# Two Fourier-attention layers on one core: x of batch 0 requested in pairs of units, first statistics of batch 1 on ScalarE, other ones and another order

## The chip, the core and the metric

The kernel runs as one program on one core of a Trainium2 chip. The metric is the time of one execution on the device, in microseconds; before the change it is 398.73 us, the median of 3 runs (398.27 to 398.82). The core has TensorE (PE, with its weight loads PEld), VectorE (DVE), ScalarE (ACT), GpSimd (POOL) and SyncE (SP). SyncE does nothing but issue DMA transfers; ScalarE issues some as well.

## The reference, cut to what matters

The input x has 2 batches, 56 channels and 128 x 128 points. Two layers of the same form, with weights of their own, are applied one after the other: x = x + layer(gn(x)). In a layer each channel is a token, a field of 128 x 128 points:

```python
# B, K, H, W, A = (2, 56, 128, 128, 8); N = batch and channel
def gn(v):       # one mean and variance for each batch and each group of 4 columns,
    ...          # over all 56 channels and all 128 rows
    return (v - mean) / sqrt(var + 1e-5)
# layer(t):
xa = t.reshape(B * K, 1, H, W)
xn = inorm(xa, g1, b1)                     # inorm: per field, over its 128 x 128 points
k, q, v = (fno_layer(xn, ...) for the K, Q and V weights)           # 8 heads each
attn = softmax(einsum('baks,bals->bakl', q, k) / sqrt(H * W))       # 56 x 56 for each head
out = fno_layer(attn @ v, P weights)
att = inorm(out + xa, gan, ban)
an  = inorm(att, g2, b2)
h   = fno_layer(an, M0 weights, norm=True, act=True)                # act: gelu
h   = fno_layer(h, M1 weights, norm=True)
y   = inorm(h, gmo, bmo) + att
# fno_layer: irfft2(complex weights times the 32 x 16 kept modes of rfft2(x)) + b,
#            inorm if norm, plus a 1x1 skip, gelu if act
```

What matters below is that the very first step of each layer, gn, needs the sums and the squares over a whole batch: until all of a batch's x is there, nothing of it can be scaled.

## The kernel before, in words

**Data.** x lies in one SBUF tile X2, for each batch as 8 *units* (n = 0 to 7), each with 8 rows of points for two halves c = 0, 1 of the planes. Half c takes partitions 64c to 64c + 55, one for a channel; partition 64c + 56 holds ones, which is why 32 partitions of X2 are set to 1.0 (`row_of_ones`) before the channels 28 to 55 are loaded over part of them. So a unit of batch 0 is loaded by pieces: channels 0 to 27 for four units at a time (448 KB), channels 28 to 55 for one or two units (112 or 224 KB), and each piece must wait for the setting to ones where it overlaps. Batch 1 is loaded by 32 pieces of 112 KB.

**First stage.** `turned(0, b, n, stats)`, noted `turn0b.n`, transposes unit n on TensorE into a pair of PSUM banks (columns become partitions), copies it to P[b], and takes its statistics for each column. Before the change VectorE does that with two bn_stats of 448 elements each, from P or, for units 6 and 7 of batch 0, from PSUM. Only units 1 and 2 of batch 0 (`SUMMED`) have them from ScalarE: a copy with a running sum, and a square over the same PSUM with a running sum. `modes_chain(0, b)`, noted `modes0b`, collects them (VectorE, unit 0 or 1 of that note), averages groups of 4 columns by a matmul with the constant `group` (modes00's unit 2), takes the power -1/2 on GpSimd, and then transforms the plane: for batch 0 with scaled transform weights `fwg`, P being scaled by four ScalarE pieces afterwards (`plane_scaled`). `gram0b`, `scores0b`, `values0b`, `soft0b`, `mix0b`, `heads0b` and `norms0b` are the attention; `gelu0b`, `hchain0b` and `end0b` the two layers behind it; `prep0` and `prep1` prepare the weights of each layer. The second layer has the same notes with a 1 (`turn10`, `modes10` and so on), and takes its statistics on ScalarE for both batches.

**Order.** The program is first recorded as a list of numbered units of work, each with the engines that may do it. `ORDER`, a long text, then fixes in which order units are issued and by which engine: a word is the step to the next unit's number and the letter of its engine (V, S, G, T for VectorE, ScalarE, GpSimd, TensorE, Q for SyncE; a small v has the next GpSimd unit wait for it). Each engine works through its part strictly in that order; between engines the dependencies are found by the framework. `PLACES` gives the PSUM bank of each intermediate. A transfer is issued by SyncE or ScalarE, and a later transfer may have to wait in the queue for an earlier one to land.

**Ones.** `awake(m)` is a matmul of a tile of ones with m columns, whose result nobody reads. `AWAKE` lists them with a number, which is only their name: `awake.108` is the one listed as 10.8. There are 84, with 26,112 columns together; each leaves two matmul records. They stand in TensorE's order between the real units.

**Constants.** The constants lie in one tile, loaded by `load_const` in parts: part 0 the identity, part 1 `fw`, `group` and `fx` (144 KB), part 2 small masks (56 KB), part 4 `gw` (64 KB), and others. The weights of layer 0 come as two pieces of 272 KB (`stage`), the scalars as two of 63 KB (`sm`).

All instructions pass through the one line L243 that issues a unit, so the profile's groups are told apart by their tiles.

Of the kernel before, what the change touches and what calls it, by code (L numbers as in the profile page):

```python
# [21 lines left out]
0V 1Q 2S 5G 1V -5Q 12S 1Q -7G 1V 7S 1Q -17S 3S 7G 1V 7S 1Q 2Q -16V 7G 1Q 7S 2S -18S 25T 3T 75Q -60T -24T 14T -2T  # L22
-5T 4T -6T 86G 47V -41G -96T 1T 36T -34T 88V -2G 10Q -12Q 6V -77T 119G -50Q 7G 3G 95G -42T 1S 2T 1S -150T 23T
61Q 109G -41T -124T 125S -61V 63T -123T -17T 121V 15V -55Q 60S -16T 8S -53Q 63T -142T 125S 2T 11V -144T 88Q 63T
-79Q 62S -33Q -94T 140V 3V -34Q 16V -135T 5T 151V -55Q 37S 17S -58Q 88G -28T 1S -62Q 129V 1v 1T 1V -230T 154S
-134T -12T 223G 2S 6T -7V 4G -107G -10Q 70v -87Q 138V -2V -134Q 138T -8T 7T 4T -112V 57G 1G -110Q 24Q 138V 1T 4T
-56V 1v -73Q 74T -26T 730G -789Q 128V 24T -15V -11V 14V -2T 3T 1T -50V 56S 6T -61v 1G 1G -108Q 109G 1G -10V -74Q
10G 126S 6T 1T -168Q 155S -54V -81Q 52S -55Q 81V 64S -62V 2T 8T 46S -158Q 167V -92V 86G -145Q 5Q 84S 66T -6S 7T
1T 1T 1T -109V 49V 1V -3V -96Q 143S -224T 82Q 141G 41S -185Q 174V -169Q -14Q 195V -4V -1V 2v 7G -206Q 68T -55Q
-92T 159T 1S 328Q -232v 231Q -230V -63V -46V 110T 2V 1G -158Q 62T 1S 116G -278T 481Q -373V 85T 2T -114Q 426Q  # L30
-505T 192S -105Q 63T -7V 12V -4S 10V 42G -51V 4T 1S 1V 98S -112T 1S 1V 198V -61G -30S -57V -2V 101T -38T 16T 5G
-1T -19S 38S -193Q -96T -15T 353T 1V 1G -344T 290T -11S -85V -2V 3T 82V 68V 2S 1S -350T 266V -162Q -112T 288T
207Q -492T 288V 1T 64V -55S -8T 66V 4T 3T -158V 88T 64v 149Q -145V 1T 4T -64V 62V 1T 4T -10V -1V 19T -173G 97V
2S -100V 164V 1T -201G 137V 1T 73S 111Q -183S 73T -88T -174V 263T 1T 1T 1T -117V -1v 105V 1T 1S 12T 1T 1T 11G
-191V 89T -23V 102S 22V -9V -14S -100V -10V 112S -207V 96V 143V -115S 119V -97T 62S 32V 1v -113S 188Q -177T 36G
45S 1T -81V 122T -39V 1G -98S 21T 1T -5T -103V 274Q -170V 100V 4V -99T -8T 1V 83S 1T 16T 3V -100T -305T 406T
-96S 72S -221v 251G 11S 60Q -76S 13T 1S -34V -76V 6T -4T 2S -3v 97G -91V 1T 1V 1G 95T 83Q -89T -312Q 227V 1T 1V
-326T 395G 15S -89V 1T 1S 4G 90T -104S 2S 13V 1V 1T 93T 1S -12V 1T 1T 67Q -149V -1v 141Q -54S 8V -1G -88T 1V
161Q -239G 218T -62S -19G 30S 1v -93T 1V 148T -55T 1S 8T 1T 1T 39V 27Q -407Q 386V 1T 5S 386G -385S 11Q -242G
135V -63V 543V 2V 1v -448T 1V 90Q -81T 60T -59V 60V -15S 18Q -1Q -16S 19T 1V -73T 1V 87Q -2Q -84T 72T 1S 1S 13T  # L40
-265G 255S 1S 13Q -138G 53v 7V -421T -26T 389G 57T 2T 79T -78V 68Q -67G 76Q 354G -358V -80T 2S -1S 43T 1S 36Q 1Q
4V 1T -75V 76S -75T 1V 1G -6V 7V 1v 82Q 1Q -2Q -50T 1S 53T 6T -7Q 2V -14S 18Q -108S 4G -442T 545Q -1Q -13S -515T
178G 349Q 5V 126Q 16Q -233T 2V -1V 2v 72S -105T 122T -530T 409S 61T 1V -28T 1V 87S 1S -102T 218Q -217S 60T 182Q
# [12 lines left out]
769T 1V 9V 15Q -797T 898S -88T 10V -9V -233Q -576T 805T 1S 1S 20T 10V 65T 1V 2T 1V -134G 5T 127T 4T -130S 60G
-59S 63Q -259Q 324T 4T -308Q 29Q 164T -15v 16S 102G 10V 1T -269Q 145T 1S 61V -50S 114V 1T 8T 1T -36G 15V -58T
71S -281Q 195V 72G 19T -131S 61G -39V 19V -14T 108T 1T -90T 82v -1S -71S 1S 80T 1T 1T -325Q 346G -129V 5T -2Q
106T -307Q 214S -19S 1S 15Q 85V 1V 36V -67V 85T -22V -21V -93S 113V 2V -167Q 41S 1S 147S -20V 17T 1S -41V 44T 1S
-135Q 183V 1T -211Q -189Q 331v 70V -94T 35T -145Q -227Q 326V -308Q 321V 93G -92G 34T -33S 1T 91V 4S -149T 70T 4T  # L60
-370Q 442S -208Q 345Q -136V 1V -254Q 107V 75V 11S 66T -68S -956T 594Q 433T -253Q 162V -6v -129Q -178Q 402V 1T 4T
-2V 1T 4T 137Q -139V 1T -82S -346Q 224Q 206V -157G -57Q 126G 97T 1T -118V 109T 1S -85G 88S -437Q 436S -117V 27V
1T 3V 1T 198Q -216v 19T 11G -202Q 282T 1T 1T -255Q -226Q 471S -246Q 260v -3T 1T 1T -267Q 238G -55V 1S 56G -252Q
157G 40V 1T 71S 32V -50V 19T -279Q 290S 1T 39T -165V -134Q 177S 1T 7T 1T 1T 91V -90T 95v -104V 5T 169Q -316Q
315Q -70S 18S -38V -1V 19G -470Q 379S 74G 1V -82T 83T 16T -15S 21V -3v 7G 63Q -164V -180Q 365Q -192V 112T 1S
-478Q 374T 93T -9V 10v 2G -91V -3S -223Q 48Q 185V -8T 2T 162Q -111S -430Q 17Q 369T 85S -91V 90T -14v -95T -389Q
402V 2S 11V -6G 101T -312Q 308T -90G -6V 7V 1V 1T 82V -101S 21V 86S 4S -9T 1T -83v 95V -1G -88T 1V 59G 99Q -240G
167T -122S 126S 1v -4S -219G 117T 1S 152Q -216G 217T 1V -142T 169Q -3Q 1Q -166V 93T 53T 1V 35Q -419Q 420Q -89S
8T 1T -105G 150T 5S 1S -157v 152S 35Q -34S 17Q -242G 170T 36V -35V -174V -150Q 332T 1T 1S 57T 1V 21Q 3Q 3Q -22T
1V 38Q -19Q -88T -45V 95T 1S 19T 1S 18Q -14S -3S 33Q -99v 70S 9T -395Q 396V 27Q -290G 268T 1V -84T 2S -1S 45T 1S  # L70
38T 1S -96T 112Q -54T -105G 62V -14V 115T -102T 2T -60G 66V 37V 38S -80V -58G 141S 1S 9T -428Q 397T 1S -5T -57G
96Q -1Q 4V 69Q -163T 83Q 2Q 3V 7T 45Q -144V 5V 1G -311Q 312V 1v 49S 5T 1V -69S -4G 110S 1S -92T -317Q 319V -32T
170Q -148T 1S -1133T 1141V 2v 92S -21T 1S -68T 1V -37S 34T 1V 90S -26T 63Q 1Q 22Q -14T -218G 214Q 3Q -70S 5T 1V
20T 1S 41Q -46T 50V -11Q 4T 1V 27Q -2Q -68S -164G 169T 1V 44T 1S 1S -220V 175T 1T 1V 56T -10S 2T -1S -46V 74Q
-251v 238T -13S 3Q 2Q 3V 3Q -58T 2S 54Q 5V -19T 1S 19T -14T -43V -2V 4V 2V 40V -43T 2T 2T 65Q -64V 1G 62Q -61V
1V -13S 81Q -6Q -13S -48G 52S 10T 1V -14S 4S -3T 1S 15Q 17Q -29T -53V 64Q -10S 13T -63T 1S 172S -28S -86Q 5V
111v -124T 1V -68G 13T 2V 66T -1315T 1320S 1S -73v 4V 80Q 76S 16G -169T 1V 60S 20T -14T 1S 7T 96G -109S -64T 65T
9Q 83S -84Q -7S 14Q 2Q -1Q 3V -8Q 2V 7T 5S -89V 173T 6V -5V 9Q -93S 87Q -107T 1V 14S 1S 69G -64T -4T 1V 69G 19Q
-18T 6V 1Q -23G -50S 1T 1V 73Q -8V 4Q -37S -31T 1T 2V 21G 5S 37Q -34G -23V 24T 6V 4Q -2Q 26Q -65S 2T 6T -1369T
1389G -23V 4T 23V 1Q 2Q 7S 39Q -38G -9Q 29Q -59S 6T 36T -35V 2V -1G 2V 33V -44S 12G 1v -1372T 1434Q 5Q -35Q 2Q  # L80
-14Q 33Q -1436T 1419V 32Q -35Q 22Q -1423T 1392Q -2Q 16Q -37T -11G 12v 38Q -36T 1V 95S -1479T 1414Q 66G -98v 4T
1V 61Q -30Q -30T 1V 70T 24T 1V -68Q -1406T 1471S 1G 5V -2Q -17S 2S 1G -11T 12T 4V 10S -25T 1V 7G 20S -1Q -37T
-1T 2T 25Q 1S -13V -1S -1Q 3Q -1453T 1460V 2S -1470T 1469Q -18V 2S -1Q -4V 2S -1446T 1445Q -1446T -2T -7T 4T 1T
1463S
# [98 lines left out]
SUMMED = (1, 2)  # L183
# [85 lines left out]
def fno_layers(ctx: ExitStack, tc: tile.TileContext, x, out, weights, small, const):  # L269
# [89 lines left out]
    def begin():  # L359
# [15 lines left out]
        for g in (0, 4):  # L375
            for c in range(2):
                load_x("QS"[c], 0, c, 0, 28, g, 4)
# [927 lines left out]
```

## Time and profile before

| | before |
|---|---|
| median of 3 runs | 398.73 us (398.27 to 398.82) |
| the profiled execution: time, span | 397.13 us, 395.3 us |
| mean granted TensorE clock | 0.978 |
| PE busy, share of the span | 371.3 us, 94% |
| DVE busy | 325.8 us, 82% |
| ACT busy | 253.1 us, 64% |
| POOL busy | 199.6 us, 50% |
| HBM read, written | 24.29 MB, 14.68 MB |
| matmuls of ones (168 records) | 63.5 us |

The durations below come from the profiled execution, and its span begins with the first instruction. A row of the timeline has the start, the length, the engine, the operation, what it writes and reads, the count of merged instructions, and in brackets the idle time before it and what ended that. Rows with ACTq or SPq are DMA transfers being issued by a queue; their length is the time in which they were issued, not the transfer's own.

### The profile page before, as it was taken

The numbers are of one execution on the slowest core, as the hardware profiler recorded it, in microseconds if no ns is written. First come the engines' busy times: TensorE is split into PE (matmuls) and PEld (weight loads), VectorE is DVE, ScalarE is ACT, GpSimd is POOL, SyncE is SP. The second block draws the span as 40 slices with busy tenths as digits, with TensorE's granted clock in tenths as the row PEclk, the third lists the DMA queues.
The fourth block names the chain that finished last, engine by engine and source line by source line (L and its number), as shares of the span: only waits on it lengthen the run. The fifth ranks groups of instructions, "written<-read, shape, count | busy, mean of one in ns | idle before, by whom it ended". The sixth has DMA issues, their size and how long they took to land.

```text
span 395.3 us, 14788 instructions
## 1 busy us (share of the span) xinstructions
PE 371.3 (94%) x6380; PEld 251.9 (64%) x6380; DVE 325.8 (82%) x583; ACT 253.1 (64%) x446; POOL 199.6 (50%) x207
## 2 busy tenths in 40 slices
PE   8789999999999999999999999999998999888895
PEld 4465687498657655667766696597575555456453
DVE  7554899999799897799869999778988888986972
ACT  0164788526947979873886798765559958993400
POOL 9942529421565566426628811434556440397460
PEclk9868999999999999999989999999999999999999
DMA  7989700300005355200120346620045324312756
GB/s 165 220 194 202 211 9 2 111 3 3 2 2 163 89 139 157 83 2 26 57 63 2 97 126 195 211 62 2 2 119 161 118 74 133 83 36 90 224 178 225
DMA packets 21317, 39.93 MB, mean 101 GB/s; under 512 B 4612, under 2 KB 5380, under 8 KB 21252
## 3 DMA queue, kind: packets, MB, share of 16 engines
q1 hardware_dynamic: 20002, 35.25, 31.6%
q10 hardware_dynamic: 1250, 3.74, 3.4%
q8 instruction: 50, 0.82, 0.9%
q14 instruction: 15, 0.12, 0.1%
HBM read 24.29 MB, written 14.68 MB: 99 GB/s over the span
## 4 chain that ended last, share of the span: by engine, by line
PE 63%; DVE 15%; ACT 9%; issue 4%; DMA 4%; POOL 3%; SPq 0%; ACTq 0%; DVEq 0%; POOLq 0%
PE psum L243 63%; ACT P L243 5%; DVE P L243 5%; DMA X<-x 3%; DVE WU L243 3%; DVE WT L243 2%; DVE X L243 2%; POOL X L243 2%; ACT psum L243 2%; DMA xr<-store 1%; DVE f L243 1%; POOL P L243 1%; ACT WT L243 1%; ACT L243 1%; SPq L243 0%
## 5 line engine op out<-in xcount | busy, mean ns | idle before, releaser
L243 PE MATMUL psum<-ones 128*128 128x256 f32 (+3 forms) x168 | 63.5, 504 | 2.0 <-DVE ones L243 1.0
L243 POOL TENSOR_TENSOR X<-X,gvr 128x1024 f32<-128x1024 f32 x20 | 47.2, 2375 | 18.8 <-DVE P L243 7.8
L243 PEld LDWEIGHTS psum<-C,P 32*128 32x128 f32 (+4 forms) x1124 | 40.4, 159 | 19.0 <-issue 4.9
L243 PEld LDWEIGHTS psum<-P 128*64 128x64 f32 (+1 forms) x1568 | 48.5, 138 | 4.9 <-ACT P L243 2.3
L243 PE MATMUL psum<-P 128*64 128x56 f32 (+1 forms) x1568 | 50.9, 223 | 0.5 <-ACT P L243 0.5
L243 PE MATMUL psum<-C,P 32*128 32x128 f32 (+4 forms) x1124 | 48.2, 252 | 2.3 <-DVE X L243 0.9
L243 DVE SCALAR_TENSOR_TENSOR X<-psum,cols,xr 128x1024 f32<-128x1024 f32 x32 | 40.1, 1270 | 5.0 <-PE psum L243 2.2
L243 PEld LDWEIGHTS psum<-ones 128*128 128x128 f32 x168 | 30.4, 213 | 21.6 <-issue 9.2
L243 ACT COPY P<-psum 128x1024 f32<-128x1024 f32 (+4 forms) x38 | 32.7, 893 | 11.8 <-PE psum L243 10.3
L243 ACT ACTIVATE P<-psum,cols 128x1024 f32<-128x1024 f32 x32 | 35.2, 1111 | 6.0 <-PE psum L243 5.5
L243 PE MATMUL psum<-X,BTx 57*64 57x512 f32 x256 | 34.6, 612 | 1.9 <-ACT psum L243 1.0
L243 ACT ACTIVATE psum<-P 128x1024 f32<-128x1024 f32 x32 | 33.0, 1031 | 0.7
L243 ACT COPY WT<-psum 128x896 f32<-128x896 f32 x30 | 26.7, 906 | 10.0 <-PE psum L243 9.7
L243 DVE STREAM_TRANSPOSE P<-psum 128x448 f32<-128x448 f32 (+1 forms) x24 | 28.8, 1230 | 2.6 <-PE psum L243 2.6
L243 POOL TENSOR_TENSOR P<-P,X 128x1024 f32<-128x1024 f32 x12 | 28.0, 2374 | 5.1 <-ACT P L243 2.9
L243 PE MATMUL psum<-P,C 128*64 128x112 f32 (+2 forms) x296 | 29.1, 381 | 1.1 <-DVE gc L243 0.4
L243 PEld LDWEIGHTS psum<-C,X 56*128 56x128 f32 x512 | 20.4, 152 | 11.7 <-issue 7.9
L243 ACT ACTIVATE P<-xf,uc 128x56 f32<-128x56 f32 x112 | 26.8, 332 | 1.5 <-PE psum L243 1.5
L243 POOL TENSOR_TENSOR X<-P,X 128x1024 f32<-128x1024 f32 x10 | 23.5, 2378 | 7.6 <-DVE P L243 4.2
L243 PE MATMUL psum<-C,X 56*128 56x56 f32 x512 | 24.4, 243 | 3.1 <-DMA X<-x 2.2
L243 ACT ACTIVATE P<-P,sh,gv 128x1792 f32<-128x1792 f32 x12 | 21.9, 1874 | 7.6 <-PE psum L243 5.3
L243 DVE SCALAR_TENSOR_TENSOR P<-P,hs,psum 128x1024 f32<-128x1024 f32 x20 | 24.6, 1272 | 2.2 <-PE psum L243 2.0
(236 smaller groups left out, 713.4 us busy)
## 6 DMA issues: line engine op xcount, KB each, us to landing
xr<-x SPq DMA_DIRECT2D x64, 112.0 KB
store<-X SPq DMA_DIRECT2D x64, 112.0 KB
xr<-store SPq DMA_DIRECT2D x64, 112.0 KB
X<-x SPq DMA_DIRECT2D x34, 112.0 KB
out<-P SPq DMA_DIRECT2D x32, 112.0 KB
out<-P SPq DMA_DIRECT2D x8, 224.0 KB
out<-P ACTq DMA_DIRECT2D x8, 224.0 KB
stage<-weights SPq DMA_DIRECT2D x4, 272.0 KB
```

What stands on the lines that cost most here:

```text
L243: done = getattr(engines[letter.upper()], method)(*args, **kw)
```

## The change

1. *x of batch 0.* SyncE asks for half c = 0 and ScalarE for c = 1, pair of units by pair: channels 0 to 27 of units 0 to 3, then channels 28 to 55 of units 0 and 1, then 2 and 3, then channels 0 to 27 of units 4 to 7, then channels 28 to 55 of 4 and 5; units 6 and 7 are asked for by SyncE alone. The settings to ones go in the same order. ScalarE's first activation (`mhalf`), which brings its table load, comes behind its second request instead of behind its last. ScalarE issues 5 transfers of x instead of 7. No transfer of batch 1, of weights or of scalars is asked for before the last of batch 0; constant part 1 is asked for after it, with eight others between.
2. *Statistics.* For batch 1 of the first layer all eight units get ScalarE's summing copy and summing square; the 16 bn_stats and their bn_aggr go, and `modes01` adds the sums up like the second layer does.
3. *Ones.* 62 instead of 84, with 20,224 columns, at other places.
4. *Order.* `ORDER` and `PLACES` are new as a whole. The units are the same but for those named. In batch 0 the units are transposed in the order 1, 0, 3, 2, 4, 5, 6, 7 instead of 2, 3, 4, 5, 0, 6, 1, 7; some other units change engine, among them four products of scores00 from GpSimd to VectorE, one set of 16 small products there from ScalarE to GpSimd and one to VectorE, and two scalings of X2 from VectorE to GpSimd.

```diff
 ORDER = """
-0V 1Q 2S 5G 1V -5Q 12S 1Q -7G 1V 7S 1Q -17S 3S 7G 1V 7S 1Q 2Q -16V 7G 1Q 7S 2S -18S 25T 3T 75Q -60T -24T 14T -2T
...
+0V 1Q 1S 1S 1S 1V 1G 1Q 1S 1V 1G 1Q 1S 1Q 1S 1V 1G 1Q 1S 1V 1G 1Q 1Q 1Q 1Q 18T -8T -2T 65G 2G 39V -103T 58V -62T
...
 AWAKE = [(0, 512)] * 9 + [
-    (10.8, 512), (14.4, 512), (15.3, 384), (17.4, 256), (18.7, 256), (20.6, 384), (23.1, 512), (24.0, 256),
...
+    (8.1, 512), (9.0, 128), (10.0, 512), (10.9, 128), (12.6, 384), (15.9, 512), (16.8, 128), (18.4, 256),
...
         clear("V", ones, 1.0)
-        for g in (0, 4):
-            for c in range(2):
-                load_x("QS"[c], 0, c, 0, 28, g, 4)
-            if not g:
-                load_const("S", 0)
+        load_x("Q", 0, 0, 0, 28, 0, 4)
+        load_x("S", 0, 1, 0, 28, 0, 4)
+        load_const("S", 0)
         S.activation(mhalf, ones[:, :2], AF.Copy, scale=-0.5)
-        for g in range(0, 8, 2):
+        for g in (0, 2):
             for c in range(2):
                 row_of_ones("VG"[c], 0, c, g, 2)
-        for g, n in ((0, 2), (2, 2), (4, 2), (6, 1), (7, 1)):
             for c in range(2):
-                load_x("QS"[c], 0, c, 28, K, g, n)
+                load_x("QS"[c], 0, c, 28, K, g, 2)
+        for c in range(2):
+            load_x("QS"[c], 0, c, 0, 28, 4, 4)
+        for c in range(2):
+            row_of_ones("VG"[c], 0, c, 4, 2)
+        for c in range(2):
+            load_x("QS"[c], 0, c, 28, K, 4, 2)
+        for c in range(2):
+            row_of_ones("VG"[c], 0, c, 6, 2)
+        for g in (6, 7):
+            for c in range(2):
+                load_x("Q", 0, c, 28, K, g, 1)
...
-        if L == 0 and b == 0 and n in SUMMED:
-            k = 72 + SUMMED.index(n)
+        if L == 0 and (b or n in SUMMED):
+            k, m = (n, 8) if b else (72 + SUMMED.index(n), 2)
             S.activation(grid(dst, 2), p[:, :, :448], AF.Copy, accum_out=acc[:, k : k + 1])
-            S.activation(p[:, :, :448], p[:, :, :448], AF.Square, accum_out=acc[:, k + 2 : k + 3])
+            S.activation(p[:, :, :448], p[:, :, :448], AF.Square, accum_out=acc[:, k + m : k + m + 1])
         elif L == 0:
             copy("SV", grid(dst, 2), p[:, :, :448])
-            k = 2 * n if b else 2 * [i for i in range(8) if i not in SUMMED].index(n)
+            k = 2 * [i for i in range(8) if i not in SUMMED].index(n)
             with work.unit():
                 for s in range(2):
-                    V.bn_stats(stats[:, k + s, :], p[:, s, :448] if b == 0 and n >= 6 else grid(dst, 2)[:, s])
+                    V.bn_stats(stats[:, k + s, :], p[:, s, :448] if n >= 6 else grid(dst, 2)[:, s])
...
-            if L == 0:
-                V.bn_aggr(mv, flat if b else flat[:, :72])
+            if L + b == 0:
+                V.bn_aggr(mv, flat[:, :72])
                 V.tensor_scalar(mv[:, 1:2], mv[:, 0:1], mv[:, 0:1], mv[:, 1:2], ALU.mult, ALU.add)
-                if b == 0:
-                    V.scalar_tensor_tensor(mv, mv, 0.75, rest, ALU.mult, ALU.add)
+                V.scalar_tensor_tensor(mv, mv, 0.75, rest, ALU.mult, ALU.add)
             else:
                 V.tensor_reduce(mv, flat[:, :16].rearrange("p (a n) -> p a n", a=2), AX.X, ALU.add)
                 V.tensor_scalar(mv, mv, 1.0 / (N * K), None, ALU.mult)
+            if L == 1:
                 V.tensor_scalar(mv[:, 0:1], mv[:, 0:1], nm0, None, ALU.add)
```

More of the change, by code (lines that the diff above doesn't have):

```diff
@@ L27 @@
[L27 to L31, printed above, removed]
@@ new lines @@
+19V -120S 119V 2V -80S 87v -127S 333Q -411Q 67T 1S 1S 343Q -212G -180Q 62T 331Q -291V 1V 57V 1G 1S 248Q -251S
+-239T 180V -37S 1S 37V -178T 2T 61Q 64T 1S 1S 111T 1S 15T 3V 1T -262T 5T 247V 16V -80V 90T 1S -16V 4V 62V -64v
+65T 1V 1G 1V 3S -1S 3G 2V 147Q -148V -249Q 93T -176T 273T 1S -280T 357T -92T 3V 1T 1T 66V -3V 7T 3T -159v 87T
+70V 1T 4T -101G 99V 1T 4T -262Q 157G 38V 1S 64V 1T 11T 1T -2V -262V 185G -96G 165V 1T -67V 1T 1S 66S 9T 1T 1T 1T
+1T 1T -94S 191Q -277V 191V -10V 9V -20S -103V -106V 314Q -106S -103V 35T -139V 35S 5V 180S 98Q -113S 16T -220V
@@ new lines @@
+24V 1G 124T -145T 1V 145S 1T 1V -138V 14Q -603T 567T 1S 1S 32Q 16T 10V 237T -250T 251S -137T -113S 1S 2V 111T 2S
+-1S -102V 4Q -20Q -36T 1S 1S 41v 247T 2V -278G 142T 3V 4V -5S -741T 631T 1S -630T 742V 132V -128V -108T 1S -8S
+9S 98V -152G 157T 2T 2T 1V 1G -139T 1S 1S -621T 759V 9G -8V 1G -751T 599T 1S -10T 1S 283V -122V 1T -13V 15V
+-141Q -13S -609T 762v 7T 1V -774T 889G -285S 291v -888T 764T 1V -769T 893T 1V -7G 8G -130T 1S 114V 21G -5V 4S
+-889T 888S -108T 10V -789T 760T 20V -19V -175Q -2Q 186V -205Q -574T 601Q -597T 600Q 222T 10V -837T 585Q 243V
@@ new lines @@
+-7Q 5V 1Q -99G -61G 164T -98G 97Q -1Q 3V -98V 60T 18S -412Q 395S -5T 1S 42T 45Q -137v -3T 1V 1G 2V 92S 1S -446Q
+407T 1V 16T -395Q 325T 2V -337Q 475Q 16Q -155V 2v 71T 58Q -61S 4S -105T 125S -124S 36T 1V -3T 1V -332Q 252G
+-259Q 409T 65Q -45S -167G 164T 45Q -5Q -439Q 298T 150T -48S 45Q -146S 150V -46T 37Q 44Q -21Q 1Q -22T 1V 25Q -64S
+1T 1V -1231T 1275T -213G -4G 222S -72V 24T 1T 48S 1T -47V -1S 42S 7S 9Q 18Q -69V 55T -2Q 1Q 2V -20S -218G 231T
+-4Q 5V -55T 2S 40T 1S 19T 5S 1S 8Q -73V 6V -2V 56S -15T 1V -48V 5T -2S 71Q -496Q 246G 256Q -73T 2T 1V 2V 64T
@@ L85 @@
+5Q -20Q -15Q 34Q -44T 1V 71T -49Q -14Q 7Q 43Q -13Q -1430T 1411V 4Q -1Q -2Q 52S 11S 1G 3T 4V 2S -1Q -29T -1456T
+1458T 23V 2S -1Q -15S -8V 1Q 1S 5G -52Q 48V 7T 1V -7Q 5G 5V 2S -4Q 1S -24T -1T 2T 4V -1449T 1451S -1Q -4V 2S 22Q
+-1464T 1441Q 13S -1458T 3T
 """
 PLACES = [int(c) for c in (
[L88 to L89 removed]
@@ L92 @@
+    "0622420246603002046550664764204460234426540020576462660620420026464"
 )]
```

106 lines of the change are left out of this document (45 added, 61 removed), and 17 rows, old and new, of the table AWAKE.

## The prediction

> **What bounds the kernel now.** I read the page first, then the chain of waits, then the head in the timeline, then tables by stretch of time.
>
> ```profile
> span 395.3 us, 14788 instructions
> ```
>
> The profiled execution took 397.13 us, so 1.8 us lie outside its span; the median of the runs is 398.73 us, 1.6 us above it. I make the sum against 397.13 and add 1.6 at the end. The chain of waits (start, length, what):
>
> ```profile
> 5.09 13.20 DMA X<-x
> 18.31 0.33 ACTq L243
> 18.68 1.28 ACT L243
> ...
> 20.17 1.70 ACT P L243 x3
> 21.92 16.37 PE psum L243 x127
> ...
> 39.39 17.39 PE psum L243 x397
> 56.81 5.14 PE psum L243 x105
> 61.96 49.52 PE psum L243 x830
> ```
>
> The head is a story of its own: until 18.6 us the chain lies in x transfers and in ScalarE's queue, which issues them; then come the table load and ScalarE's first copies, then TensorE. From 39.4 to 111.5 us TensorE hardly pauses. The timeline of the head:
>
> ```profile
> 2.55 16.10 ACTq L243 DMA_DIRECT2D X<-x  x7
> ...
> 29.84 1.11 PE L243 MATMUL psum<-C,X 56*128 56x56 f32 x16
> 30.88 3.44 PE L243 MATMUL psum<-ones 128*128 128x256 f32 x6
> 30.98 1.16 DVE L243 BATCH_NORM_STATS2 stats<-psum 128x6 f32<-128x448 f32 x2 [2.16 <-PE psum L243]
> ...
> 34.25 0.71 PE L243 MATMUL psum<-C,X 56*128 56x56 f32 x16
> 34.89 0.38 PE L243 MATMUL psum<-mv,C 128*128 128x2 f32 x2
> ...
> 37.28 1.71 PE L243 MATMUL psum<-P,fwg 128*32 128x448 f32 x16
> ```
>
> ScalarE spends 16.1 us issuing seven requests for x, because a request waits in its queue until an earlier one has landed. Its copies stand behind that, so the last of batch 0's eight transposed units starts at 29.84 us, and the matmul that averages the statistics (psum<-mv,C, in modes00) only at 34.89, behind three ones (30.88 to 34.3) and the first unit of batch 1. The first scaled transform (psum<-P,fwg) follows at 37.28. These two are my milestones. By stretches (length, then busy time of PE, PEld, DVE, ACT, POOL, then granted clock, DMA share, GB/s):
>
> ```profile
> 0.00:20.00 20.00, 16.40 (x65) 8.78 (x65) 12.65 (x10) 1.31 (x2) 18.75 (x14) 0.91 0.84 192
> 20.00:40.00 20.00, 18.41 (x165) 11.76 (x169) 10.93 (x27) 10.22 (x17) 6.89 (x17) 0.74 0.87 199
> 40.00:60.00 20.00, 19.97 (x448) 15.59 (x448) 18.00 (x49) 15.51 (x28) 8.70 (x25) 1.00 0.39 103
> 60.00:80.00 20.00, 20.00 (x235) 11.43 (x235) 19.18 (x43) 12.96 (x28) 12.41 (x16) 1.00 0.19 56
> 80.00:100.00 20.00, 20.00 (x519) 17.48 (x520) 18.84 (x29) 9.54 (x21) 4.00 (x4) 1.00 0.01 3
> ```
>
> The DMA engines are full (share 0.84 and 0.87) for 40 us, at 192 and 199 GB/s; afterwards VectorE is busy 90 to 96% beside a full TensorE, part of which are ones. In the head what matters is which bytes come first; behind it, TensorE and VectorE together.
>
> **The head: x by pairs, the table load first.** Batch 0 of x is 56x128x128 floats, 3.67 MB; with the identity (64 KB) 3.73 MB. Before, a piece of batch 1, weights and constants were mixed in. Now nothing else is asked for ahead of batch 0. At 192 GB/s it is moved by 3.73/0.192 = 19.4 us. From the last byte to the waiting engine I allow 2 us, an estimate (0 to 4: no row shows it alone): 21.4. ScalarE issues five requests for x instead of seven, its table load comes ahead of most of them, and it is free long before. The mean cannot come right then: the request for the "group" constant used to be SyncE's eighth and now stands behind eight others that follow batch 0. Their sizes:
>
> ```profile
> X<-x SPq DMA_DIRECT2D x34, 112.0 KB
> stage<-weights SPq DMA_DIRECT2D x4, 272.0 KB
> ...
> C<-const_all SPq DMA_DIRECT2D x1, 144.0 KB
> sm<-small SPq DMA_DIRECT2D x2, 63.0 KB
> C<-const_all ACTq DMA_DIRECT2D x1, 64.0 KB
> C<-const_all SPq DMA_DIRECT2D x1, 64.0 KB
> C<-const_all SPq DMA_DIRECT2D x1, 56.0 KB
> ```
>
> Two pieces of weights, two of x, two of small, three constants (64, 56 and its own 144 KB): 1158 KB, 1.19 MB. So 4.92 MB must be in: 3.84 MB by 20 us, 1.08 MB more at 199 GB/s is 5.4 us: 25.4, with the 2 us 27.4. The other way to the mean is shorter: last transposes at 21.4 + 1.1, then three ones of 1280 columns (the three at 30.88 have 1280 too, 3.44 us) make 25.9. So psum<-mv,C starts at 27.4 instead of 34.89. To psum<-P,fwg it is 2.4 us as before; one unit of batch 1 now stands between them, whose last request lies three requests (336 KB, 1.7 us) behind the constant: 29.1 plus its 0.71. I take 30.3 against 37.28: **-7.0**. With no landing lag -9; with 4 us, and TensorE late behind ones at half clock, -4. SyncE's queue pays: units 6 and 7 are asked for by SyncE alone, which delays batch 1's requests; bytes, not issues, set their time, and the units wanted early (0 and 3) are asked for first, so I cost that at nothing. If unit 7, wanted near 39 us, is late, everything behind it on TensorE waits, about 1 us.
>
> ```profile
> 24.00:32.00 8.00, 8.00 (x75) 5.98 (x74) 4.49 (x9) 4.24 (x8) 2.80 (x3) 0.50 0.81 189
> ```
>
> TensorE ran this stretch at clock 0.50, although it was busy throughout. The Trainium skill, "TensorE: Matmul & The Clock Gate", Part 1, says that the clock falls to half after an idle window of about 3.4 us and comes back after a busy one; a full 8 us at half are longer than that. By the rule the new wait for x of units 4 and 5 would leave the three ones at half clock, and without it they would take less. Both end before the constant lands, so the sum stays.
>
> **First statistics of batch 1 on ScalarE.** VectorE loses the 16 bn_stats of batch 1; each of the eight units becomes a summing copy and a summing square on ScalarE, as two units of batch 0 already are:
>
> ```profile
> 28.86 0.92 ACT L243 ACTIVATE P<-psum 128x896 f32<-128x896 f32 x1 [2.19 <-PE psum L243]
> ...
> 30.61 0.19 ACT L243 ACTIVATION_READ_ACCUMULATOR psum<-psum 128x1 f32 x1
> ...
> 42.33 3.66 ACT L243 ACTIVATE P<-P,sh,gv 128x1792 f32<-128x1792 f32 x2 [5.30 <-PE psum L243]
> 45.89 0.51 ACT L243 COPY xf<-psum 128x448 f32<-128x448 f32 x1
> ...
> 59.10 6.10 DVE L243 BATCH_NORM_STATS2 stats<-P 128x6 f32<-128x448 f32 x11
> 65.23 0.59 DVE L243 BATCH_NORM_AGGREGATE mv<-stats 128x2 f32<-128x96 f32 x1
> ```
>
> A pair holds ScalarE from 28.86 to 30.80: 1.94 us. From the first scale of P (42.33) to batch 1's aggregate (65.23) it was 22.9 us, led by VectorE. In the new order ScalarE has there four scales (4 x 1.83), three copies at 0.51 to 0.56 (1.6), seven pairs (13.6) and four small ones (some 1.0): 23.5 us; its 16 small products of scores00 there have gone to POOL. What is queued behind a square: the next copy, and so the pair of PSUM banks that TensorE needs, now held 1 us longer.
>
> ```profile
> 42.30:65.20 22.90, 22.87 (x503) 18.84 (x501) 20.98 (x47) 19.64 (x37) 12.96 (x24) 1.00 0.26 68
> ```
>
> ScalarE was busy 19.64 of 22.90 there, 86%. Never idle, the new stretch is 0.6 us longer than the old; at 86% it takes 27.4, 4.5 longer. Below zero is out, since the work alone exceeds the old stretch. I take **+2.0**, in the middle.
>
> **Fewer ones, and the new order.**
>
> ```profile
> L243 DVE BATCH_NORM_STATS2 stats<-P 128x6 f32<-128x448 f32 x24 | 13.2, 610 | 6.7 <-ACT P L243 6.6
> ...
> L243 DVE TENSOR_TENSOR P<-uc,xf 128x896 f32<-128x896 f32 x7 | 7.5, 1084 | 0.5 <-PE psum L243 0.5
> ...
> L243 PE MATMUL psum<-ones 128*128 128x256 f32 (+3 forms) x168 | 63.5, 504 | 2.0 <-DVE ones L243 1.0
> ```
>
> 84 ones (168 records, 63.5 us) become 62; in columns 26,112 become 20,224, which at 2.4 ns a column is 14 us. Counted in the two orders: to the first unit of batch 1 24 become 22; on to the soft01 transposes 15 become 8; on to hchain01 13 become 5; to modes10's first transform 15 stay 15; to the end 17 become 12. A one that fills a gap costs nothing, so its going brings nothing unless TensorE is the later engine. Between 56.8 and 111.5 us it is on the chain: there ten become seven, some 0.7 us each: up to -2.1. VectorE bounds the same stretch: 16 x 0.61 = 9.8 us leave it, five products at 1.08 (four of POOL's, one of ScalarE's) come, some scalings and preparations go to POOL and others come: by 138 us it has done 3 to 5 us less. The two covers overlap; I take **-2.0** for both, from 0 to -5. The second layer has no bn_stats and the same matmuls and copies in another order: 0, from -4 to +4, no row decides it.
>
> Sum: -7.0 + 2.0 - 2.0 = -7.0; 397.13 becomes 390.1, on the median's footing **391.7 us**.
>
> **The rivals.**
> *The ones were on the path everywhere.* Then the 12 us behind the head come off whole: -7 + 2 - 12 = -17: 381.7 us. For it: TensorE is full in every row from 40 us on. Against: VectorE at 90 to 96% has little room to follow.
> *The head gains little.* Only bytes count: batch 0 was complete soon after ScalarE's last request at 18.31, so if the landing lag is nearer 4 us and the ones run at half clock, the head gains 3: -3 + 2 - 2 = -3: 395.7 us. This is also the case in which pairs side by side do not do what they are for, ScalarE's requests waiting for landings as before. The Trainium skill, "DMA: Bandwidth & Descriptors", Rules for kernel authors, says that spreading transfers over queues brings no bandwidth, since all run on the same 16 engines; the share of 0.84 agrees.
> *ScalarE becomes the bound, and it is slower.* Place: batch 1's transposes, first scale to last square. If ScalarE is busy there only as in 40 to 80 us, (15.51 + 12.96)/40 = 71%, its 23.5 us take 33.0, 10.1 more than before; TensorE waits for banks, and the gain from ones is void: -7 + 10.1 = +3.1: 401.8 us. It decides from the point where the stretch exceeds 22.9 + 7.0 = 29.9 us. For it: each pair is fed by one transposed unit that TensorE reaches in order between prep0, gchain00 and ones. Against: the products that sat in this stretch of ScalarE are gone.
>
> **How the numbers follow.** About 0.2%, 0.8 us, is what a measurement here can tell from no change. The forecast has 0.50, ones on the path 0.13, the small head 0.17 (of it 0.04 within 0.2%), ScalarE bound 0.18, nothing at all 0.02. So faster 0.50 + 0.13 + 0.13 = 0.76, same 0.06, slower 0.18. The forecast's own range, from its terms, is 387 to 395.5; to hold 8 in 10 it reaches down toward the first rival and up toward the last: 384 to 401.
>
> **What would show it.** Right: ScalarE's first copy near 11 us instead of 20; psum<-mv,C at 26 to 29 us with DMA as what came last; psum<-P,fwg near 30; no bn_stats behind the head; first scale to last square 24 to 27 us; ones 124 records. Wrong: psum<-mv,C after 31 us; that stretch over 29.9 us, with TensorE waiting for ACT; a granted clock under 0.9 after 40 us where ones have gone; or the lead of 7 us at 30 us shrinking in the second layer, where I have no term.

## The result, and the profile after

The changed kernel took 385.75 us (median of 4 runs, 383.67 to 390.38) against 398.77 us: the ratio is 0.9659 (0.9614 to 0.9703). Run again beside other kernels it gave 385.91 us against 398.40, ratio 0.9683 (0.9644 to 0.9723). A ratio, here and below, is against the kernel before on the same chip and compares the runs of each kernel within 1.5% of its fastest; one run of the kernel before at 390.74 us raises three of the ratios below (1.0080, 0.9985 and 0.9894), where the medians of all runs say more. So 12.5 to 13 us are gone, where the prediction had 7.0; 391.7 us was forecast, with 384 to 401 as the range.

The profiled execution took 385.07 us, with this span and head of the chain of waits (start, length, what):

```profile
span 383.2 us, 14690 instructions
0.73 6.79 POOL X L238 x4
7.52 11.45 DMA X<-x
...
20.75 2.05 DVE stats L238 x4
22.80 3.58 DMA X<-x
...
33.31 22.91 PE psum L238 x504
56.33 25.30 PE psum L238 x459
```

ScalarE's queue and table load have left the chain; what stands there is the setting to ones, x, and VectorE's statistics (the transfer from 22.80 is already one of batch 1). The timeline of the changed kernel's head:

```profile
4.30 3.58 ACTq L238 DMA_DIRECT2D X<-x  x3
...
12.23 0.91 ACT L238 COPY P<-psum 128x896 f32<-128x896 f32 x1 [8.91 <-PE psum L238]
...
19.11 1.17 PE L238 MATMUL psum<-C,X 56*128 56x56 f32 x31 [1.86 <-DMA X<-x]
...
20.77 1.65 PE L238 MATMUL psum<-ones 128*128 128x384 f32 x2 [0.50 <-ACT P L238]
...
23.39 2.07 PE L238 MATMUL psum<-ones 128*128 128x512 f32 x2
...
25.39 1.11 PE L238 MATMUL psum<-C,X 56*128 56x56 f32 x16
...
26.43 2.72 PE L238 MATMUL psum<-ones 128*128 128x512 f32 x6
26.60 1.16 DVE L238 BATCH_NORM_STATS2 stats<-psum 128x6 f32<-128x448 f32 x2 [1.95 <-PE psum L238]
...
28.75 0.16 DVE L238 SCALAR_TENSOR_TENSOR mv<-mv,rest 128x2 f32<-128x2 f32 x1
28.96 0.30 PEld L238 LDWEIGHTS psum<-mv,C 128*128 128x128 f32 x2 [0.65 <-DVE mv L238]
28.98 0.37 PE L238 MATMUL psum<-mv,C 128*128 128x2 f32 x2
...
31.19 1.71 PE L238 MATMUL psum<-P,fwg 128*32 128x448 f32 x16 [0.24 <-DVE fwg L238]
```

ScalarE has issued its last request by 7.9 us and copies from 12.23 instead of 20.08. psum<-mv,C comes at 28.98 (34.89 before), psum<-P,fwg at 31.19 (37.28 before). What released the mean is in brackets: VectorE's mv, not a constant; the three ones ahead of it (26.43) end at about the same time. By stretches (columns as in the prediction):

```profile
0.00:20.00 20.00, 17.09 (x126) 10.10 (x127) 14.88 (x13) 4.28 (x7) 18.77 (x14) 1.00 0.83 207
20.00:40.00 20.00, 18.90 (x187) 9.56 (x185) 13.50 (x38) 11.89 (x18) 11.98 (x35) 0.83 0.85 223
40.00:60.00 20.00, 19.87 (x436) 16.72 (x432) 17.58 (x41) 18.96 (x38) 5.42 (x3) 1.00 0.31 68
60.00:80.00 20.00, 20.00 (x388) 13.98 (x387) 18.05 (x43) 9.15 (x12) 7.51 (x6) 1.00 0.17 48
80.00:100.00 20.00, 19.65 (x408) 15.94 (x406) 18.14 (x39) 16.55 (x49) 7.18 (x6) 1.00 0.01 3
```

Between 40 and 60 us ScalarE is now the busiest beside TensorE (18.96; before 15.51). The two groups of the change:

```profile
L238 PE MATMUL psum<-ones 128*128 128x256 f32 (+3 forms) x124 | 47.8, 507 | 1.9 <-DVE ones L238 1.1 <-ACT P L238 0.5 <-ACT psum L238 0.3
L238 DVE BATCH_NORM_STATS2 stats<-P 128x6 f32<-128x448 f32 x8 | 4.5, 616 | 2.0 <-ACT P L238 1.9
```

124 records of ones are left of 168, and 8 bn_stats from P of 24. The next table follows the same units through the profiled executions: the start in us of TensorE's matmul that begins each stage, matched by its place in the order. "first layer ends" is the second layer's first transform.

| | first scaled transform | batch 1: mean | batch 1: transform | gelu01 | hchain01 | first layer ends | hchain11 | last product | span |
|---|---|---|---|---|---|---|---|---|---|
| before | 37.28 | 66.19 | 73.55 | 143.34 | 191.97 | 219.46 | 356.29 | 385.75 | 395.3 |
| changed | 31.19 | 61.04 | 66.83 | 134.26 | 180.88 | 207.42 | 345.38 | 372.96 | 383.2 |
| head alone | 28.62 | 57.56 | 64.92 | 134.69 | 183.32 | 208.85 | 345.02 | 376.77 | 386.2 |
| head and statistics, old order | 30.55 | 66.04 | 73.40 | 143.45 | 192.07 | 217.63 | 353.85 | 386.24 | 395.6 |
| changed, statistics as before | 30.48 | 76.22 | 82.01 | 149.54 | 195.81 | 222.35 | 358.32 | 386.43 | 396.8 |
| changed, head as before | 37.36 | 68.51 | 74.30 | 142.18 | 188.46 | 215.84 | 351.23 | 378.77 | 389.2 |
| before with fewer ones | 37.78 | 66.44 | 72.93 | 143.30 | 191.61 | 217.50 | 354.50 | 385.00 | 394.4 |

In the changed kernel the lead is 6.1 us at the first transform, 6.7 at batch 1's, 9.1 at gelu01, 11.1 at hchain01, 12.0 at the end of the first layer, 10.9 at hchain11, and 12.8 at the last product: half comes from the head, nearly all the rest from the first layer behind it, and 0.8 from the second.

### The profile page after: what moved, and what is told of

Read it like the earlier page. It is cut to its first block, busy times and chain, and to the rows that moved or that the text cites. A ratio compares the mean times of both kernels' runs of the same rounds, so it can differ in the third digit from the quotient of the medians.

```text
span 383.2 us, 14690 instructions
## 1 busy us (share of the span) xinstructions
PE 356.0 (93%) x6336; PEld 244.5 (64%) x6336; DVE 318.1 (83%) x570; ACT 253.6 (66%) x453; POOL 208.9 (55%) x206
## 4 chain that ended last, share of the span: by engine, by line
PE 49%; DVE 22%; ACT 13%; issue 5%; DMA 5%; POOL 4%; DVEq 0%; POOLq 0%; ACTq 0%
PE psum L238 49%; DVE P L238 10%; ACT P L238 9%; DMA X<-x 5%; DVE X L238 3%; DVE WU L238 3%; ACT psum L238 3%; POOL X L238 2%; DVE WT L238 2%; POOL P L238 1%; ACT WT L238 1%; DVE f L238 1%; DVE stats L238 1%; POOL rs L238 0%; ACT L238 0%
## 5 line engine op out<-in xcount | busy, mean ns | idle before, releaser
L238 POOL TENSOR_TENSOR X<-X,gvr 128x1024 f32<-128x1024 f32 x21 | 49.6, 2376 | 16.6 <-DVE D L238 8.4
L238 PEld LDWEIGHTS psum<-C,P 32*128 32x128 f32 (+4 forms) x1124 | 41.5, 162 | 19.6 <-issue 5.8
L238 PE MATMUL psum<-C,P 32*128 32x128 f32 (+4 forms) x1124 | 49.4, 255 | 3.3 <-DVE X L238 0.8
L238 PE MATMUL psum<-ones 128*128 128x256 f32 (+3 forms) x124 | 47.8, 507 | 1.9 <-DVE ones L238 1.1
L238 ACT COPY P<-psum 128x1024 f32<-128x1024 f32 (+4 forms) x31 | 25.8, 848 | 26.2 <-PE psum L238 23.5
L238 POOL TENSOR_TENSOR X<-P,X 128x1024 f32<-128x1024 f32 x11 | 25.9, 2377 | 16.8 <-DVE P L238 12.4
L238 ACT ACTIVATE P<-psum 128x896 f32<-128x896 f32 (+1 forms) x30 | 26.0, 867 | 10.4 <-PE psum L238 7.7
L238 PEld LDWEIGHTS psum<-ones 128*128 128x128 f32 x124 | 22.1, 207 | 16.9 <-issue 8.9
L238 PEld LDWEIGHTS psum<-C,X 56*128 56x128 f32 x512 | 19.1, 143 | 12.0 <-issue 6.0
L238 PE MATMUL psum<-C,X 56*128 56x56 f32 x512 | 22.5, 232 | 2.2 <-DMA X<-x 1.9
```

The costliest lines, as they stand in the source:

```text
L238: done = getattr(engines[letter.upper()], method)(*args, **kw)
```

## The experiments

### The head alone

```diff
 # the kernel before, with begin() of the changed kernel (requests for x, ones' rows, mhalf);
 # ORDER: the changed one up to the first unit of psum<-P,fwg with its 22 ones, then the old one
```

> The kernel before with the changed kernel's requests for x, its order up to the first scaled transform and its 22 ones there; from then on the order, the ones and the statistics of before. By the two traces psum<-P,fwg should come 6.1 us earlier than before. If the lead stays, as the prediction's sum has it: 391.5 to 393. If it is given back to VectorE and the ones later: 395 to 398.7.

Measured: 388.25 us against 398.38, ratio 0.9737 (0.9688 to 0.9787). That is 10 us, more than expected. The timeline of TensorE:

```profile
26.39 0.38 PE L239 MATMUL psum<-mv,C 128*128 128x2 f32 x2
28.62 1.71 PE L239 MATMUL psum<-P,fwg 128*32 128x448 f32 x16 [0.16 <-DVE fwg L239]
```

The first transform is 8.7 us earlier than before and the lead does not shrink: the table has 8.6 at every stage up to hchain01. It then becomes 10.6, with the same ones and the same order as before. There the kernel before had a stretch at a low granted clock:

```profile
200.00:205.00 5.00, 5.00 (x12) 2.44 (x12) 2.42 (x12) 4.16 (x9) 0.91 (x2) 0.66 0.32 100
```

A third of 5 us is 1.7 us, most of the 2.0. So the head brings 8.7 us of earlier start in that execution; what comes on top goes with the clock, which also took 1.6 us back near the end (0.50 from 355 to 360 us). By the medians the changed kernel (385.91) is 2.3 us faster than the head alone, and the intervals of the two ratios overlap: most of the whole gain is the head's.

### x by one queue, before and after

```diff
-load_x("QS"[c], 0, c, ...)      # and load_x("S", ...)
+load_x("Q", 0, c, ...)          # the order of the requests kept
```

> The kernel before with ScalarE's seven requests for x made by SyncE, in the same order; ScalarE keeps the one for the identity. If ScalarE's queue held the head of before (its first copy at 20.08 us stands behind those requests): psum<-mv,C at 29 to 31 instead of 34.9 us and 392.5 to 395. If the order of the bytes held it: psum<-mv,C not before 34 us, 397.5 to 399.

> The changed kernel with ScalarE's five requests for x made by SyncE, in the same order. If only the order of the bytes counts (the prediction's sum): level within 1 us, 384.5 to 386.5, psum<-mv,C within 1 us of the changed kernel's. If two queues side by side bring x sooner, because one queue waits for landings in turn: psum<-mv,C 2 to 5 us later, 387 to 390.

Measured: before with one queue 392.66 us against 398.40, ratio 0.9835 (0.9799 to 0.9872); changed with one queue 386.46 us, ratio 0.9687 (0.9639 to 0.9735), level with the changed kernel's 0.9683. The timeline of the kernel before with SyncE asking for all of x:

```profile
0.72 12.21 SPq L240 DMA_DIRECT2D X<-x  x14
...
16.49 0.92 ACT L240 ACTIVATE P<-psum 128x896 f32<-128x896 f32 x1 [13.84 <-PE psum L240]
...
30.04 0.35 PE L240 MATMUL psum<-mv,C 128*128 128x2 f32 x2 [0.32 <-issue]
```

and its clock in the stretch that ran at 0.50 before:

```profile
25.00:30.00 5.00, 4.72 (x56) 2.84 (x52) 4.74 (x11) 3.12 (x7) 3.03 (x4) 1.00 0.89 228
```

ScalarE waits for TensorE now, not for its own queue, and copies from 16.49 instead of 20.08, 3.6 us earlier; the mean comes 4.85 us earlier, the rest of it at the full clock. So a compute engine that must issue requests which wait for landings held the head of before, and more than half of the head's gain (5.7 of 10 us) is that engine's release. What makes the other 4 us no run separates: the order of the requests, the order of the transposed units, the head's ones and some units on other engines come together in the head alone. Side by side or not is nothing: with one queue the changed kernel is as fast (its mean comes at 29.74, 0.8 us later). The Trainium skill, "DMA: Bandwidth & Descriptors", Rules for kernel authors, has it that more queues bring no bandwidth and save issue time only; the second run agrees, and the first shows whose issue time it was worth saving.

### The constant asked for first

```diff
 # ORDER of the changed kernel: load_const("Q", 1) directly behind the last request for x of batch 0
```

> The changed kernel with constant part 1 (fw, group, fx; 144 KB) asked for right behind the last request for x of batch 0, ahead of the eight others that stand there. If its landing sets psum<-mv,C, as the prediction's sum for the head has it: psum<-mv,C 1 to 1.5 us earlier at the same granted clock in the head, and 383.5 to 384.5. If VectorE's last statistics set it (in the changed kernel's trace its weight load waits for VectorE's mv): psum<-mv,C no earlier, level with the changed kernel, 384.5 to 386.5, or later by up to 0.75 us where the 144 KB at 192 GB/s push back the first x of batch 1.

Measured: 385.40 us against 397.86, ratio 0.9679 (0.9626 to 0.9731): level with the changed kernel. In that execution mv was ready as in the changed kernel (28.92), and the mean came later, not earlier, directly behind its three ones, which ran at half clock here (4.21 us instead of 2.72):

```profile
26.43 4.21 PE L236 MATMUL psum<-ones 128*128 128x512 f32 x6
...
28.76 0.16 DVE L236 SCALAR_TENSOR_TENSOR mv<-mv,rest 128x2 f32<-128x2 f32 x1
...
30.48 0.28 PE L236 MATMUL psum<-mv,C 128*128 128x2 f32 x2
```

The constant's landing is not what the mean waits for: by the landing events in the traces it was in at 19.9 us here, and at 25.0 in the changed kernel, 3.9 us ahead of mv.

### The statistics, each in the other's order

```diff
 # changed kernel, statistics as before: turned() and modes_chain() of before;
-    S.activation(p[:, :, :448], p[:, :, :448], AF.Square, accum_out=...)   # batch 1
+    V.bn_stats(stats[:, k + s, :], grid(dst, 2)[:, s])                     # in the square's place
 # head and statistics, old order: the kernel of the head alone with
+    S.activation(p[:, :, :448], p[:, :, :448], AF.Square, accum_out=...)   # right behind the copy
```

> The changed kernel with the statistics of batch 1 of the first layer by bn_stats on VectorE again, in the places of the squares on ScalarE; all else as changed. By the prediction (+2.0 for ScalarE's pairs, -1 or so of the -2.0 for VectorE) it should be 1 us faster to level: 384.5 to 386. If VectorE's freed 9.8 us made the gain between 60 and 140 us, 3 to 6 us slower: 388.5 to 391.5.

> The kernel of the head alone, with the statistics of batch 1 of the first layer on ScalarE as well (each square right behind its copy); the order behind the head, the ones and the engines of all other units as before. The prediction's terms: +2.0 for ScalarE's pairs, some -1 for VectorE: 1 us above the head alone, 0.975 to 0.979 of before (388.5 to 390). If VectorE was what held the stretch from 50 to 110 us: 3 to 5 us less than the head alone, 383 to 385, as the changed kernel. If the statistics pay only together with the new order: within 1 us of the head alone or up to 4 us slower.

Measured: the changed kernel with its old statistics 400.29 us against 398.38, ratio 1.0042 (1.0013 to 1.0071), some 14 us slower than the changed kernel. The head with the new statistics in the old order 397.07 us against 397.60 by the medians of all runs, ratio 1.0080 (1.0006 to 1.0155), no faster than before and some 9 us slower than the head alone. Both expectations were far too mild. The second one first, ScalarE's timeline, then the stretch from the first scale to the last square, then what TensorE waited for in it:

```profile
47.42 3.83 ACT L239 ACTIVATE P<-xf,uc 128x56 f32<-128x56 f32 x16 [0.86 <-PE psum L239]
51.15 0.90 ACT L239 ACTIVATE P<-psum 128x896 f32<-128x896 f32 x1
```

```profile
35.60:64.30 28.70, 25.42 (x496) 20.79 (x498) 11.45 (x29) 25.94 (x54) 12.57 (x24) 0.88 0.46 103
55.00:60.00 5.00, 5.00 (x83) 4.31 (x83) 0.00 (x0) 3.21 (x8) 3.42 (x3) 0.55 0.00 0
```

```profile
PE psum L239 <- ACT psum L239: 2.3, 2, 2.0
```

In the old order ScalarE still has its 16 small products (3.83 us) in front of the copies and squares. TensorE waits for banks, its clock falls to 0.55, VectorE stands still for 5 us, and the stretch takes 28.7 us instead of 22.9. The lead, 6.7 us at this run's first transform, is 0.15 at batch 1's mean. In the changed order the same stretch has no such products:

```profile
36.30:59.80 23.50, 23.37 (x496) 19.09 (x494) 20.36 (x48) 22.46 (x39) 8.40 (x15) 1.00 0.41 94
```

ScalarE is busy 22.46 of 23.50 us and TensorE hardly waits (busy 23.37). And the new order with VectorE's statistics (two stretches, and TensorE's waits from 50 to 70 us):

```profile
50.00:70.00 20.00, 12.35 (x113) 8.91 (x109) 14.10 (x28) 4.43 (x9) 3.96 (x3) 0.56 0.01 2
70.00:75.00 5.00, 5.00 (x20) 2.21 (x22) 4.96 (x7) 0.00 (x0) 0.00 (x0) 0.50 0.00 0
```

```profile
PE psum L236 <- DVE stage L236: 6.3, 2, 5.4
```

VectorE has the bn_stats beside the products that it took over; TensorE waits 6.3 us for it and runs at about half clock for 25 us. Batch 1's mean comes at 76.22 instead of 61.04. The bn_stats were put where the squares stood and nothing else was moved, so this is the price of the undoing in this order, not of bn_stats as such. Together the two runs show that, of these two orders, the new statistics pay in the new one only, and the new order with the new statistics only. That the 16 small products alone make the difference is not shown, since the two orders differ in more.

### The rest without the head

```diff
 # the changed kernel with begin() of before; ORDER: the old one with its ones up to the first unit of
 # psum<-P,fwg, then the changed one; copy and square of batch 1's unit 0 on ScalarE
```

> The changed kernel with the requests for x, the order and the ones of before up to the first scaled transform; statistics, order and ones as changed from there. If the parts add: the head's share (0.974) taken out of the whole (0.967), 0.993 of before, 395 to 397. If the head's gain is only to be had once, with the rest worth as much without it: 390 to 392. psum<-P,fwg near 37 us in either case.

Measured: 393.57 us against 397.60 by the medians of all runs, 4.0 us faster, between the two expectations; ratio 0.9985 (0.9915 to 1.0055), which leaves open whether the rest pays by itself. The profiled execution has no lead at the first transform and 7.0 us at the last product. By medians the parts add roughly: 10 us for the head, 4 for the rest, 13 for both.

### The ones

```diff
 # before with fewer ones: 7 of 15, 8 of 13 and 5 of 17 left out behind the head, 5,376 columns;
 # before with no late ones: all 60 behind the first unit of batch 1 left out, 17,536 columns
-    awake(m)
```

> The kernel before with 20 of its 84 ones left out (5,376 columns), so that each segment behind the first unit of batch 1 holds as many as the changed kernel has there (8, 5, 15, 12); everything else in place. The prediction's term (ones and freed VectorE together -2.0, from 0 to -5): 396 to 398. If the ones were on TensorE's path wherever the next real matmul begins as a one ends (in the trace of before that is so for nearly all of them up to 340 us), the 20 hold it for about 11 us, and of that 7 to 11 us come off: 388 to 392. If the rest of the new order made the gain, nothing: 398 to 399.

> The kernel before with none of the 60 ones behind the first unit of batch 1 (17,536 columns; they hold TensorE for 38 us in the trace of before). Ones on the path: 20 to 35 us less, 364 to 379. Ones in gaps that the other engines leave: 0 to 5 less, 394 to 399. Ones that keep the clock up: without them the granted clock falls where TensorE waits (200 to 215 and behind 360 us), and the time rises to 400 to 405.

Measured: with fewer ones 396.72 us against 398.38, ratio 0.9973 (0.9941 to 1.0006): not told apart from before. With none 402.44 us, ratio 1.0095 (1.0059 to 1.0130): slower. In the table the kernel with fewer ones is level with before up to hchain01 (143.30 and 191.61 against 143.34 and 191.97), although 15 of the 20 that went stood ahead of that; its 2 us appear behind hchain01, where nothing was taken out and where its clock stayed up:

```profile
200.00:205.00 5.00, 4.85 (x37) 2.97 (x36) 3.62 (x16) 4.68 (x11) 0.55 (x1) 1.00 0.31 100
```

Without any late ones the clock falls where TensorE waits:

```profile
205.00:215.00 10.00, 5.77 (x42) 4.57 (x38) 7.33 (x23) 6.58 (x15) 2.01 (x3) 0.66 0.19 59
220.00:225.00 5.00, 3.70 (x72) 3.21 (x69) 4.07 (x4) 5.00 (x5) 5.00 (x3) 0.56 0.13 41
```

So leaving out ones that end exactly where a real matmul begins brought nothing behind the head: what these runs fit is that the real matmul waits for the other engines, and that the one stands in this wait. The ones of the head stayed in both runs. There two of them stand between the arrival of x and the last transposes (20.77 and 23.39, 3.7 us at half clock in the changed kernel), and what they cost was not tried.

### Filling TensorE's waits

```diff
 # the changed kernel, ORDER and AWAKE:
+    (400.0, 512), (401.0, 512)        # filled: two ones ahead of turn00.4
+    (128 to 512) x 8                  # kept: these two, and eight in waits between 285 and 358 us
```

> The changed kernel itself once more, as the level that the next three are held against: 0.966 of the kernel before, 384 to 386.

> The changed kernel with two more ones of 512 columns ahead of turn00.4, where TensorE waits 1.9 us for x and after which its granted clock is 0.5 from 21 to 27 us in the changed kernel's trace. If that wait brings the clock down: the clock stays at 1.00 until 40 us, psum<-mv,C comes at 26.4 as in the run of the head alone instead of 29.0, and the time is 2 to 3 us less: 382 to 383.5. If the landing of x bounds the head: level, 385 to 386, psum<-mv,C at 28 to 29. If the two ones hold up turn00.4: 386 to 387.

> The changed kernel with ten ones more: the two of the run before that filled the head's wait for x, and eight (128 to 512 columns, 2,304 together) in TensorE's waits of 0.5 to 1.5 us between 285 and 358 us, where the traces of the changed kernel show granted clocks of 0.74 to 0.9 in one execution or another. If those waits bring the clock down: mean clock 0.99 or more, 380 to 383, with a smaller spread. If the clock falls for another reason: clock 0.98 and 384 to 387. If the ones hold up the matmuls behind them: 386 to 390 at a clock of 0.99.

Measured: the changed kernel 385.91 us against 398.40, ratio 0.9683 (0.9644 to 0.9723); filled 386.07 us, ratio 0.9639 (0.9584 to 0.9695), its runs three from 382.77 to 384.02 at mean clocks of 0.988 to 0.992 and three from 388.12 to 390.01 at 0.975 to 0.981: not told apart. Kept 395.78 us against 397.60 by the medians of all runs, ratio 0.9894 (0.9788 to 1.0000): slower than the changed kernel, at mean clocks from 0.961 to 0.986, as no expectation had it. The stretches of the first profiled execution of the changed kernel, and then of the filled one:

```profile
17.00:21.00 4.00, 1.65 (x40) 1.41 (x36) 2.07 (x4) 1.19 (x2) 3.26 (x7) 0.91 0.90 198
21.00:24.00 3.00, 3.00 (x19) 1.70 (x20) 2.47 (x5) 3.00 (x6) 2.40 (x6) 0.50 0.68 218
24.00:27.00 3.00, 3.00 (x19) 1.43 (x18) 1.05 (x3) 1.17 (x3) 0.86 (x1) 0.50 0.83 214
```

```profile
17.00:21.00 4.00, 3.44 (x37) 1.97 (x38) 2.10 (x4) 1.21 (x2) 2.63 (x3) 1.00 0.92 201
21.00:24.00 3.00, 3.00 (x37) 1.57 (x36) 3.00 (x6) 3.00 (x6) 2.82 (x9) 1.00 0.79 221
```

and its timeline of TensorE:

```profile
26.50 0.38 PE L236 MATMUL psum<-mv,C 128*128 128x2 f32 x2
```

Filled, TensorE is busy 3.44 of 4 us instead of 1.65, the clock stays at 1.00 and the mean comes at 26.50 instead of 28.98, as expected. But in that execution the clock fell later instead, to 0.50 between 290 and 300 us, and the time is that of the changed kernel. The kept kernel was meant to mend that and did not; its timeline of TensorE (this execution is one of its longer ones):

```profile
286.47 1.09 PE L236 MATMUL psum<-X,BTx 57*64 57x512 f32 x8 [0.51 <-ACT psum L236]
289.29 0.79 PE L236 MATMUL psum<-ones 128*128 128x128 f32 x2 [1.73 <-ACT psum L236]
```

The one did not fill the wait of 0.69 us that stood here: it waited 1.73 us itself, for ScalarE to release the PSUM bank it was given. TensorE was busy 2.76 of the 5 us from 285 to 290, and its clock was 0.50 from 290 to 295. That this wait and others like it make the whole of the 10 us is not shown. No version beat the changed kernel.

## Why the prediction was right, and where its sizes were off

**The head, -7.0.** Right in kind and nearly in size: -6.1 at the first transform of the profiled execution, -7.8 (29.50) in a second one, -8.7 in the run of the head alone. The step that failed is the one that named the last arrival. The sum let the constant set the mean at 27.4 us and gave the other way, through the statistics, 25.9. Measured, that other way set it, and later than the sum had it. The bytes were right: by the landing events in the trace, x of batch 0 was in at 19.8 us (19.4 in the sum) and the constant at 25.0 (25.4). The lag of 2 us that was added to both is shown by no run: the transposes at 19.11 began 0.14 us after the landing they waited for (7.52 + 11.45 in the chain). But the last transposes come at 25.39 instead of 21.4, behind other transposed units and two ones that ran at half clock; the prediction had named this half clock and set it aside, because it let the constant come last. From there to the mean it is 3.6 us. In these the three ones of the sum (26.43 to 29.15) and VectorE's last bn_stats (26.60) with the chain of small steps to mv (28.91), for which the sum had no term, end almost together: mv released the mean here, the ones did with the constant moved to the front, which did not bring the mean forward. The mean's 28.98 us in this execution was 27.27 in the second one and 26.39 in the head alone; the sum's 27.4 lies among them by luck, with a lag that was not there in place of TensorE's and VectorE's work that was.

**The rival of the small head.** It held that only bytes count and that ScalarE's requests did not matter. The first half holds after the change (one queue or two is the same), the second does not: taking the requests off ScalarE's queue alone brought 5.7 us (0.9835) with the order of the bytes unchanged.

**The statistics, +2.0.** The stretch is 23.5 us, +0.6, the lower bound: ScalarE was busy 96% of it, not 86%. That the sum's 23.5 us of work is the stretch to the tenth is luck: the work was 22.46 us, with 1.04 of idle time. The rival in which ScalarE becomes the bound is real and its place was right: in the old order it happens (28.7 us), and the small products that left this stretch, which the prediction named against it, are the difference that the rows show; that they alone decide is argued.

**Ones and VectorE, -2.0.** From the first transform to gelu01 the lead grew by 3.0; less the 0.6 for the statistics the term is -3.6. Mis-sized, and the ones have no part in it that these runs can show: with as many left out of the kernel before, nothing moved there. VectorE's work between these two stages is 91.21 us instead of 95.92, 4.7 less, within the 3 to 5 that the prediction had; with the fewer ones alone it was 95.89. So I put the gain down to VectorE's freed time and the order that goes with it; the two runs that separate them both lose the gain, and which of the two makes it is open. The rival of ones on the path everywhere (381.7 us) came nearer to the measured time than the forecast did, but for a wrong reason: left out of the kernel before, all 60 late ones made it slower.

**The stretch from gelu01 to the end of the first layer.** No term: the sum ended the effect of ones and VectorE by 138 us. The lead grew there by 3.0. Of that 2.0 us come without the new order: the head alone, with the ones and the order of before there, gains as much, and so does the kernel with fewer ones; neither has the 5 us at clock 0.66, which make 1.7 of it. The other 1.0 I put down to the order, which no run isolates.

**The second layer, 0.** 0.8 us, within its -4 to +4.

**What was to show it.** ScalarE's first copy (12.23), psum<-P,fwg near 30 (31.19), the stretch of 24 to 27 us (23.5) and 124 records of ones came as said or nearly; psum<-mv,C came at the upper end, with VectorE and not a DMA ahead of it. The sign that would have made it wrong, a granted clock under 0.9 behind 40 us, did show (0.76 from 325 to 330 us) without costing the gain.

The sum of -7.0 is thus short by 3.0 in ones, VectorE and statistics (1.4 of it the statistics), 3.0 in the stretch that had no term and 0.8 in the second layer, against 0.9 too much in the head.

## What to carry to other kernels

Look at which engine issues transfers ahead of its own first work: if its requests wait for landings, its queue is on the path even when the bytes are not, and moving the requests to an engine that does nothing else is a small edit with a large part of the gain. Work moved between two full engines is to be judged with what already stands in the target's stretch: the same squares lengthened their stretch by 0.6 us in an order that had moved ScalarE's other work away, and by 5.8 us in the one that had not. That a filler ends as real work begins is no proof that it delays it; leave some out and see.

## What the runs showed of the hardware

**The granted clock falls for waits much shorter than I had thought, and not every time.** In the changed kernel waits of 1.9 and 0.5 us within 4 us (busy 1.65 of 4.00) were followed by 6 us at 0.50. The head alone has the same waits and kept 1.00:

```profile
17.00:21.00 4.00, 1.75 (x39) 1.46 (x36) 2.18 (x4) 1.31 (x2) 3.37 (x7) 1.00 0.87 209
```

The Trainium skill, "TensorE: Matmul & The Clock Gate", Part 1, has the activity window of some 3.4 us run freely, so that it falls differently on the same work; the two rows agree with that. They also show that no wholly idle window is needed, as the prediction had quoted the rule: the longest wait was 1.9 us.

**Much of the spread between runs goes with the clock.** Five of the six runs of the head alone went from 385.78 us at a mean clock of 1.000 over 387.73 to 388.52 at 0.987 to 389.37 at 0.985; five of the six of the changed kernel with one queue from 383.94 at 0.994 to 389.44 at 0.971. About 2.4 us go with each hundredth of the mean clock in both, and some 3 with the sixth run (394.29 at 0.974, 396.50 at 0.952). It is not all: two runs of the kernel before took 395.28 us at 0.977 and 398.77 at 0.978. A difference of 2 us between two single executions of these kernels therefore says little unless the clock is read beside it.
